# Expert results in seven places, the last sums of batch 0 behind the values, and gathers that begin two turns sooner, on one Trainium2 core

## The chip, the cores and the metric

The kernel runs on one NeuronCore of one Trainium2 chip, as one program with one launch. The metric is the device time in microseconds from the start to the end of an execution; less is better. The engines are TensorE (PE in the profile, with PEld for its weight loads), VectorE (DVE), ScalarE (ACT), GpSimd (POOL) and SyncE (SP), which only issues transfers. Each engine works its own instructions off in the order in which the program hands them over, and waits at the head of its queue for the semaphores of the instruction there. Transfers (DMA) are issued from SP, ACT and POOL; those issued from POOL here are indirect ones, in which a table of indices in on-chip memory names the row of each partition.

## What is computed

Two layers on an input of 2 images, 256 channels and 56 x 56 places (3136 tokens an image), all in float32. The first is a grouped non-local block. The second, which takes most of the time, is causal attention with four heads and then a mixture of experts in which each token takes its best two of eight:

```python
# layer 1, t: tokens (2, 3136, 256)
t = t + attention(layernorm(t), W_attn, W_proj)      # causal, 4 heads of 64

def _L1_ffn_ref(x, gate_w, gate_b, W1, b1, W2, b2):  # x = layernorm(t)
    logits = xf @ gate_w + gate_b
    probs = jax.nn.softmax(logits, axis=-1)
    top2_vals, top2_idx = jax.lax.top_k(probs, 2)
    cw = jnp.zeros((N, Ee), dtype=xf.dtype).at[jnp.arange(N)[:, None], top2_idx].add(top2_vals)
    def step(acc, params):
        w1, bb1, w2, bb2, we = params
        h = jax.nn.gelu(xf @ w1 + bb1, approximate=False)
        y = h @ w2 + bb2
        return (acc + we[:, None] * y, None)

t = t + ffn(layernorm(t))
x = _from_tokens(t, x)                               # back to (2, 256, 56, 56)
```

The hidden width of an expert is 512.

## The kernel before

**Attention.** For each batch b, stripe i of 448 query columns (seven of them) and pair of heads hp (two), the loop goes over chunks j of 128 keys. Step n computes the scores (`scores`, L806 on TensorE), ScalarE takes their exponential (L810), VectorE adds the results up into a tile `acc` (L829), and three steps later (LAG) `values(n - LAG)` multiplies them by the values into the PSUM tile `yp` (L857). When a stripe is finished, ScalarE copies `yp` out (L867) and POOL adds its halves (L868). `sum_rows` multiplies `acc` by ones (tile `sp`, L878) to get the row sums of the softmax; `store_sums` copies them (L889), sends them to memory and asks for their inverses four steps later. A table `visits` says at which step the sums of each stripe are taken. At every stripe but the first, the sums stand ahead of `values` in the order of the instructions, and `values` then copies `yp` into the `acc` tile that the sums have just been read from; for a stripe whose sums are not yet taken the copy goes to a tile of the tag "st" instead, of which there are five. The banks of `yp` are shared by the stripes, so the next stripe's values wait for the copy.

**The experts.** The 2 x 3136 x 2 pairs of token and expert are sorted by expert into 105 blocks of 128 slots, of which 102 can be filled (MAIN). Blocks 0 to 41 hold tokens of batch 0 alone; 42 to 56 hold tokens of both batches (MIXED is 57); 57 to 101 hold tokens of batch 1. Turn n of the loop works on several blocks at once: `hidden(n)` (16 matmuls, L1673, and ScalarE's GELU, L1682), `inputs` (transposes, L1650), `weights` (a copy of the expert's first matrix by VectorE, L1661), and `outputs` of the block three turns back (8 matmuls into `yp`, L1692; two VectorE additions of the bias into `ys`, L1702). The three last blocks are brought closer: two turns back and then one.

`ys` is one of three tiles of pool `es` that the blocks take in turn. For blocks below 57 SP sends it to the table `y_slots` (L1707). For blocks 42 to 98, POOL scatters its rows to `y_tokens` (L1713), by tokens of batch 1. The last three blocks (99 to 101) keep `ys` on the chip: TensorE places them with a matrix of ones and zeros, `hots` (L1784), which is made with one POOL iota for each block (L1854) and compared later.

**The finish.** Two generators run beside the experts and give one step at a time when they are pulled; the function `meanwhile` pulls them once in each turn. `finish(0)` brings batch 0's tokens together after block 56: `fetch` loads the rest of the sum for a pair of 128-token chunks (SP, L1871) and issues four gathers out of `y_slots` (POOL, L1878), `add` makes four VectorE additions (L1913), and `store` transposes the pair on TensorE (`yo`, L1927), copies it on ScalarE into one of two tiles `ot` (L1932) and sends it to the output (SP, L1933). 25 chunks take 50 gathers. `gathered[0]` counts the gathers of the present turn and is set back in each turn; `since` is the turn in which the generator began. `finish(1)` goes ahead of it in the queue and does the same for batch 1 with plain loads (L1898) out of `y_tokens`. `last_rows` loads the last rows of batch 1 (L1752); `store_last` (L1803) sends what the last three blocks placed.

The pool `bg` holds attention's row buffers, two each of the tags "xr" and "xn". Their last users are the early rows that the experts' blocks 0 to 5 read.

The order within each engine is the order of the program text, as the schedule is manual: what stands first in the code stands first in its queue.

Of the kernel before, what the change touches and what calls it, by code (L numbers as in the profile page):

```python
# [10 lines left out]
F32 = mybir.dt.float32  # L11
# [17 lines left out]
def conv_attn_moe_kernel(  # L29
# [51 lines left out]
    nc = tc.nc  # L81
    P = 128
    B, C, N = x.shape
    NH = C // P
# [9 lines left out]
    NB = N // W  # L94
# [11 lines left out]
    OFF = 16 * N  # L106
# [4 lines left out]
    GB = 3  # L111
# [9 lines left out]
    LAST = max(n for n in range(NCH) if complete(n) <= DIRECT)  # L121
    REST = N - LAST * P
# [65 lines left out]
    with tc.tile_pool(name="c_w", bufs=1) as cw, tc.tile_pool(name="c_s", bufs=2) as cs, tc.tile_pool(  # L188
        name="c_big", bufs=5, space=PSUM
    ) as cbig, tc.tile_pool(name="c_acc", bufs=1, space=PSUM) as cacc:  # L190

        xr = [cw.tile([P, NCH, C + 2], F32, name=f"xr{b}") for b in range(B)]
# [8 lines left out]
        for b in range(B):  # L201
            for col in (0, C + 1):
                nc.gpsimd.memset(xr[b][:, :, col : col + 1], 1.0)
            n = 0
# [54 lines left out]
        def channels():  # L259
# [12 lines left out]
            base=0, pattern=[[-D, G], [0, D]], channel_multiplier=1,  # L272
# [3 lines left out]
            base=D - 1, pattern=[[D, G], [0, D]], channel_multiplier=-1,  # L276
# [234 lines left out]
    def layer1(nm, general):  # L511

        with ExitStack() as whole:
# [195 lines left out]
            def attend(qT, kT, v, fst, fs, psc, py, open_batch, visit, between, clock, later, finished):  # L709
# [240 lines left out]
                for n in range(len(steps) + LAG):  # L950
                    copy_sums = None
                    if n in visits:
                        visit(*visits[n])
                        b, i, hp = visits[n]
                        if i == 0 and hp + 1 == NH:
                            turn_rows(b, 1)
                        if i > 0 and visits[n] != final:
                            copy_sums = sum_rows(b, hp, i)
                        aligned()
                    if n + 1 < len(steps) and n > LAG and steps[n][2] == 0 and steps[n - LAG - 1][2] == 0 and steps[n - LAG - 1][4]:  # L960
                        if steps[n][1] > 1:
                            turn_rows(*steps[n][:2])
                    if n < len(steps):
                        b, i = steps[n][:2]
                        if n == 0 or steps[n - 1][0] != b:
                            open_batch(b)
                        between(b, i, ends[b, i] - n, (steps[n][3] + 1) * P > i * W + 1, room(n))

                    late = n >= LAG and steps[n - LAG][4]
                    if n >= LAG:  # L970
                        due(clock[0])
                        clock[0] += 1
                    if n >= LAG and not late:
                        values(n - LAG)
                    if n in visits and visits[n][1] == 0:
                        copy_sums = sum_rows(b, hp, 0)
                    if copy_sums:
                        copy_sums()
                    if n < len(steps):
                        scores(n)  # L980
                    if late:
                        values(n - LAG)
# [595 lines left out]
            def experts(w1s, w2s, b2s, ex, es, ps6, between, amid, need, written, settle, decide):  # L1578
# [108 lines left out]
                def outputs(n, state):  # L1687
                    g, to = state
                    e = ids[n]
                    yp = ps6.tile([P, 512], F32, tag="yp", bufs=2, name=f"yp_{nm}_{n}")  # L1690
                    for k in range(KH):
                        nc.tensor.matmul(  # L1692
                            yp[:, :C],
                            g[:, k, :],
                            w2s[k][:, bass.ds(e, 1), :].rearrange("p e d -> p (e d)"),
                            start=(k == 0),
                            stop=(k == KH - 1),
                        )
                    ys = es.tile([P, C], F32, tag="ys", name=f"ys_{nm}_{n}")
                    for c in range(NH):  # L1700
                        part = slice(c * P, (c + 1) * P)
                        nc.vector.tensor_tensor(  # L1702
                            ys[:, part], yp[:, part],
                            b2s[c][:, bass.ds(e, 1), :].rearrange("p e d -> p (e d)"), ALU.add,
                        )
                    if n < MIXED:
                        nc.sync.dma_start(out=y_slots[n * P : (n + 1) * P], in_=ys)  # L1707
                    if n >= FULL0:
                        if n >= DIRECT:
                            direct[n] = ys  # L1710
                            worked[0] = n + 1
                            return
                        s = nc.gpsimd.indirect_dma_start(  # L1713
                            out=y_tokens,
                            out_offset=bass.IndirectOffsetOnAxis(
                                ap=to[:, n % GB : n % GB + 1], axis=0
                            ),
                            in_=ys,
                            in_offset=None,
                            bounds_check=2 * N - 1,  # L1720
                            oob_is_err=False,
                        )
                        group = f"y_tokens_{nm}"
                        tc.declare_no_dep(s.ins, group=group, reason="different rows")
                        tc.add_to_no_dep_group(group, s.ins)
                        scattered.append((n, s.ins))
                    worked[0] = n + 1
                    if n == MIXED - 1:
                        written()
# [119 lines left out]
                        ids.extend(experts_of(len(ids) // GB))  # L1849
                    between()  # L1850

            def number_columns(a):

                nc.gpsimd.iota(  # L1854
                    hots[a], pattern=[[1, REST]], base=LAST * P - OFF, channel_multiplier=0,
                    allow_small_or_imprecise_dtypes=True,
                )

            def finish(b, oy, bufs):

                t = ts[b]
# [1 line left out]
                def fetch(n, m, k):  # L1863

                    ys = [
                        oy.tile([P, 2, C], F32, tag=f"y{b}{c}", bufs=bufs, name=f"y{c}_{nm}{b}_{n}")
                        for c in range(2)
                    ]
                    res = oy.tile([P, 2, C], F32, tag="res", bufs=bufs + 1, name=f"res_{nm}_{n}")
                    rows = res[:k, :m]  # L1870
                    nc.sync.dma_start(out=rows, in_=rest_d[:k, n : n + m])  # L1871
                    ahead.append((n, m, k, ys, rows))
                    for c, y in enumerate(ys):
                        for a in range(m):
                            while gathered[0] == (1 if turn[0] < since + 4 else 2 - (turn[0] % 4 == 0)) or turn[0] < since + 2:
                                yield False
                            gathered[0] += 1
                            nc.gpsimd.indirect_dma_start(  # L1878
                                out=y[:k, a],
                                out_offset=None,  # L1880
                                in_=y_slots,
                                in_offset=bass.IndirectOffsetOnAxis(
                                    ap=idxs[b][:k, c, n + a : n + a + 1], axis=0
                                ),
                                bounds_check=MIXED * P - 1,
                                oob_is_err=False,
                            )
                            yield True
# [48 lines left out]

                ahead, added, since = deque(), None, turn[0]
                parts = deque(pairs())
                steps = deque(range(GB))  # L1940
                if b:
                    parts = deque([(0, 1, P), *pairs(1, LAST)])
                while b == 0 and (parts or ahead):
                    if parts:
                        yield from fetch(*parts.popleft())
                        if len(parts) % 2 == 0 and steps:
                            number_columns(steps.popleft())
                    if len(ahead) == bufs or not parts:
                        now = ahead.popleft()
                        yield from add(*now)  # L1950
                        if added:
                            while stored[0]:
                                yield False
                            store(*added)
                            yield True
                        added = now
# [296 lines left out]
            with ExitStack() as moe:  # L2253
# [23 lines left out]
                def written():  # L2277
                    spread_rows.close()
                    oy = pool(moe, "oy", bufs=2, side="right")
                    last_pool.append(oy)  # L2280
                    hot = pool(moe, "hot", bufs=1, side="right")
                    hots.extend(hot.tile([P, REST], F32, name=f"hot{a}_{nm}") for a in range(GB))
                    queue.append(finish(0, oy, 2))
                    queue.appendleft(finish(1, oy, 3))

# [203 lines left out]
```

## Time and profile before

| What | us |
|---|---|
| median of three runs | 1267.23 |
| their least and greatest | 1265.88, 1269.42 |
| the profiled execution | 1266.76 |
| its span, first to last instruction | 1264.9 |

The profile comes from one execution; its span leaves out what lies ahead of the first instruction and behind the last, 1.9 us here. The granted TensorE clock is 0.999 of full speed on the mean. The share of each slice (a fortieth of the span, 31.6 us) that an engine was busy, in tenths:

```profile
PE   8999999999999999999999999999999999999997
DVE  2582567666676574566677888785744443455563
ACT  0255555565656555465555656563334333343432
POOL 1103231110021103211111656000266012666650
DMA  9996101000000000100000223641344433556653
```

Batch 0's attention ends near 475 us, batch 1's near 850; then come the experts. POOL's busy slices 23 to 25 and 29 to 31 hold the scatters of tokens to x_slots, batch 0's and then batch 1's. POOL's busy stretch near the end (slices 35 to 39, from about 1075 us) holds the gathers of batch 0.

The windows view gives the busy time of each engine in a stretch (the columns are the stretch, its length, and for each engine its busy time with the number of instructions, then the granted clock, the share of the DMA engines and GB/s). The first is with one scatter a block, the second the first eight turns with gathers, the third the rest of them:

```profile
1020.00:1077.00 57.00, 57.00 (x399) 53.85 (x399) 21.87 (x64) 21.02 (x75) 14.58 (x15) 1.00 0.37 108
1077.00:1107.00 30.00, 30.00 (x210) 28.07 (x209) 12.60 (x36) 10.89 (x40) 19.25 (x18) 1.00 0.52 158
1107.00:1210.00 103.00, 99.13 (x698) 91.69 (x697) 59.13 (x160) 42.35 (x138) 69.40 (x65) 1.00 0.67 206
```

A line of the waits reads: engine, what it did next, its line, what ended the wait, then us in total, times, and the longest. In the timeline a row is the start, the time it took, the engine, line, operation, what it writes and reads, how often, and in brackets the idle time before it with its releaser.

### The profile page before, as it was taken

To read this page: it belongs to the slowest core of one execution; us is meant where nothing else is said; L and a number is where in the kernel's file an instruction comes from. 1 tells how busy PE (TensorE), PEld (TensorE's weight loads), DVE (VectorE), ACT (ScalarE), POOL (GpSimd) and SP (SyncE) were. 2 spreads that over 40 slices of the span, in tenths; PEclk is the share of its full clock that TensorE was granted. 3 is DMA by queue.
4 is the path that set the end of the run, shared out by engine and by line. 5 is a ranking of instruction groups with operands and counts; after the bars stand their busy time and mean duration, and the time that the engine had idled before them with its cause. 6 is when DMAs were issued, how large, how long until landed. Compare 5 with 4: busy or idle time off the path is not lost.

```text
span 1264.9 us, 28755 instructions
## 1 busy us (share of the span) xinstructions
PE 1242.6 (98%) x10881; PEld 848.1 (67%) x10881; DVE 772.8 (61%) x1687; ACT 610.7 (48%) x1237; POOL 348.9 (28%) x318
## 2 busy tenths in 40 slices
PE   8999999999999999999999999999999999999997
PEld 8876655555454545655555444479889999988886
DVE  2582567666676574566677888785744443455563
ACT  0255555565656555465555656563334333343432
POOL 1103231110021103211111656000266012666650
PEclk9999999999999999999999999999999999999999
DMA  9996101000000000100000223641344433556653
GB/s 316 352 344 194 28 24 38 25 15 26 14 17 16 1 26 21 35 23 13 9 16 25 72 67 115 218 119 60 101 143 148 121 106 92 161 180 207 208 169 116
DMA packets 119875, 125.93 MB, mean 100 GB/s; under 512 B 28375, under 2 KB 109640, under 8 KB 119730
## 3 DMA queue, kind: packets, MB, share of 16 engines
q1 hardware_dynamic: 109074, 97.45, 25.3%
q0 software_dynamic: 9840, 25.67, 6.1%
q8 instruction: 90, 1.47, 0.5%
q10 hardware_dynamic: 816, 0.88, 0.2%
q14 instruction: 55, 0.45, 0.1%
HBM read 62.06 MB, written 61.05 MB: 97 GB/s over the span
## 4 chain that ended last, share of the span: by engine, by line
PE 47%; DVE 2%; issue 1%; ACT 0%; DVEq 0%
PE ht_f L1673 14%; PE yp_f L1692 13%; PE sc_f L806 7%; PE yp_f L857 7%; PE tp_f L1650 2%; PE pp_f L682 1%; PE yo_f L1927 1%; DVE y_f L1913 1%; PE qk_f L613 1%; PE v_f L628 0%; PE tail_f L1784 0%; DVE acc_f L829 0%; PE sp_f L878 0%; ACT st_f L810 0%; PE bp_f L1405 0%
## 5 line engine op out<-in xcount | busy, mean ns | idle before, releaser
L810 ACT ACTIVATE st_f<-sc_f 128x896 f32<-128x896 f32 (+5 forms) x400 | 331.2, 839 | 189.7 <-PE sc_f L806 164.4
L829 DVE TENSOR_TENSOR acc_f<-acc_f,st_f 128x896 f32<-128x896 f32 (+6 forms) x344 | 343.9, 1000 | 105.3 <-ACT st_f L810 93.2
L806 PE MATMUL sc_f<-qT_f,kT_f 64*64 64x448 f32 (+5 forms) x3136 | 345.3, 499 | 0.5 <-issue 0.3
L857 PE MATMUL yp_f<-st_f,v_f 64*64 64x448 f32 (+4 forms) x2896 | 323.5, 511 | 1.1 <-ACT acc_f L867 0.6
L806 PEld LDWEIGHTS sc_f<-qT_f,kT_f 64*64 64x64 f32 x3136 | 140.7, 133 | 133.6 <-issue 108.1
L1682 ACT ACTIVATE g_f<-ht_f,b1b 128x128 f32<-128x128 f32 x408 | 116.5, 371 | 226.1 <-PE ht_f L1673 111.4
L857 PEld LDWEIGHTS yp_f<-st_f,v_f 64*64 64x64 f32 x2896 | 122.5, 133 | 129.1 <-issue 105.0
L1673 PE MATMUL ht_f<-xT_f,w_f 128*128 128x128 f32 x1600 | 196.2, 275 | 4.0 <-issue 3.9
L1673 PEld LDWEIGHTS ht_f<-xT_f,w_f 128*128 128x128 f32 x1600 | 192.8, 192 | 8.8 <-issue 4.7
L1537 POOL DMA_INDIRECT x_slots<-xr_f,idx x100 | 113.6, 1136 | 148.4 <-DVE xr_f L1535 75.0
L868 POOL TENSOR_TENSOR qT_f<-acc_f 128x448 f32<-128x448 f32 x22 | 25.5, 1161 | 380.3 <-ACT acc_f L867 380.2
L1661 DVE COPY w_f<-w1s_f 128x1024 f32 x102 | 71.4, 701 | 86.0 <-PE ht_f L1673 38.6
L584 POOL TENSOR_SCALAR xn_f<-t 128x256 f32<-128x256 f32 (+1 forms) x50 | 80.3, 1613 | 130.0 <-DVE t L185 44.1
L1713 POOL DMA_INDIRECT y_tokens<-ys_f,to_f x57 | 59.6, 1046 | 126.4 <-DVE ys_f L1702 100.8
L1702 DVE TENSOR_TENSOR ys_f<-yp_f,kT_f 128x128 f32<-128x128 f32 x102 | 29.4, 289 | 96.6 <-PE yp_f L1692 63.6
L613 PE MATMUL qk_f<-px_f,wat 128*128 128x512 f32 (+2 forms) x224 | 87.2, 541 | 0.6 <-ACT px_f L605 0.6
L613 PEld LDWEIGHTS qk_f<-px_f,wat 128*128 128x128 f32 x224 | 40.6, 190 | 39.7 <-issue 33.7
L1692 PE MATMUL yp_f<-w2s_f,g_f 128*128 x204 | 60.9, 379 | 0.5 <-issue 0.5
L1692 PE MATMUL yp_f<-px_f,g_f 128*128 x204 | 61.1, 381 | 0.0
L1878 POOL DMA_INDIRECT y_f<-y_slots,idx x50 | 56.6, 1132 | 15.3 <-issue 15.3
L1692 PE MATMUL yp_f<-kT_f,g_f 128*128 x204 | 60.7, 379 | 0.0
L1692 PE MATMUL yp_f<-v_f,g_f 128*128 x204 | 60.7, 379 | 0.0
(299 smaller groups left out, 1308.0 us busy)
## 6 DMA issues: line engine op xcount, KB each, us to landing
x_slots<-fill SPq DMA_DIRECT2D x1, 8190.0 KB
xb_f<-x_slots SPq DMA_DIRECT2D x60, 130.0 KB
x_slots<-fill SPq DMA_DIRECT2D x1, 7296.0 KB
y_slots<-ys_f SPq DMA_DIRECT2D x57, 128.0 KB
kept<-t SPq DMA_DIRECT2D x2, 3200.0 KB
x<-in_x_dram SPq DMA_DIRECT2D x14, 448.0 KB
rb_f<-inverses SPq DMA_DIRECT2D x56, 112.0 KB
y_f<-y_tokens SPq DMA_DIRECT2D x23, 256.0 KB
```

Of the source, the lines that this page charges most:

```text
L584: nc.gpsimd.tensor_scalar(xn[:k, a], ts[b][:k, n + a, :C], ts[b][:k, n + a, MEAN : MEAN + 1], ts[b][:k, n + a, RSTD : RSTD + 1], ALU.subtr ...
L613: nc.tensor.matmul(ps[:, :w], wat[:, c, d0 : d0 + P], px[:, s % 2, c, :w], start=(c == 0), stop=(c == NH - 1),)
L806: nc.tensor.matmul(to, left, right, start=True, stop=True)
L810: nc.scalar.activation(st[rows, :, c0:], ps[rows, :, c0:W], AF.Exp, scale=SCALE)
L829: nc.vector.tensor_tensor(acc[rows, :, c0:], acc[rows, :, c0:], st[rows, :, c0:], ALU.add)
L857: nc.tensor.matmul(to, left, right, start=first, stop=end)
L1537: s = nc.gpsimd.indirect_dma_start(out=xds[b], out_offset=bass.IndirectOffsetOnAxis(ap=idxs[b][:kk, k, n : n + 1], axis=0), in_=xr[:kk], i ...
L1661: nc.vector.tensor_copy(w, w1s[:, :, bass.ds(e, 1), :].rearrange("p c e h -> p c (e h)"))
L1673: nc.tensor.matmul(ht[:, k, :], w[:, c, k * P : (k + 1) * P], xT[:, c, :], start=(c == 0), stop=(c == NH - 1),)
L1682: nc.scalar.activation(g[:, k, :], ht[:, k, :], AF.Gelu, bias=b1bs[b][:, k, i : i + 1])
L1692: nc.tensor.matmul(yp[:, :C], g[:, k, :], w2s[k][:, bass.ds(e, 1), :].rearrange("p e d -> p (e d)"), start=(k == 0), stop=(k == KH - 1),)
L1713: s = nc.gpsimd.indirect_dma_start(out=y_tokens, out_offset=bass.IndirectOffsetOnAxis(ap=to[:, n % GB : n % GB + 1], axis=0), in_=ys, in_o ...
```

## The change

It has four parts.

1. In attention, the sums of (batch 0, stripe 6, second pair of heads) are put behind `values(n - LAG)`, as those of stripe 0 already are. So at that stripe the copy of `yp` no longer goes to the `acc` tile but to one of tag "st".
2. `ys` goes round seven places, by the block's number modulo 7: the three tiles of tag "ys", the two of tag "xr" and the two of tag "xn".
3. The gathers of batch 0 begin in the first turn instead of the third. For eight turns there is one a turn, and then one and two in turn; before there were, after two turns without, one a turn for two turns, and then two a turn, but one in each fourth. The number of gathers is the same.
4. The three iotas that number the columns of `hots` are issued together where the pool is opened, behind block 56's outputs, rather than between the gathers.

No matmul, addition or transfer is added or removed. Since later gathers mean later additions, the transposes and stores of batch 0's pairs 20, 22 and 24 move, too. At the end the order of transfers in SP's queue is, before and after (rows of batch 1 have odd numbers, of batch 0 even ones):

```
before  ... out 20, out 22, out 24, load 17 x2, out 15, last rows x4, load 19 x2, out 17, hot
after   ... rest 24, load 17 x2, out 15, last rows x4, load 19 x2, out 20, out 22, out 17, out 24, hot
```

The transposes of 20 stand ahead of `hidden(100)`, those of 22 ahead of `hidden(101)`, and those of 24 behind those of 17. The last gathers stand between the scatters of blocks 95 and 96.

```diff
@@ attend
-                        if i > 0 and visits[n] != final:
+                        short = i == 0 or (i, hp) == (NB - 1, NH - 1)
+                        if i >= 0 and not short:
                             copy_sums = sum_rows(b, hp, i)
...
                     if n >= LAG and not late:
                         values(n - LAG)
-                    if n in visits and visits[n][1] == 0:
-                        copy_sums = sum_rows(b, hp, 0)
+                    if n in visits and short and visits[n] != final:
+                        b, i, hp = visits[n]
+                        copy_sums = sum_rows(b, hp, i)
                     if copy_sums:
                         copy_sums()
@@ outputs
-                    ys = es.tile([P, C], F32, tag="ys", name=f"ys_{nm}_{n}")
+                    home = n % 7
+                    ys = (es if home < 3 else bg).tile(
+                        [P, C], F32, tag="ys" if home < 3 else "xr" if home < 5 else "xn", name=f"ys_{nm}_{n}"
+                    )
@@ finish
-            def number_columns(a):
-
-                nc.gpsimd.iota(
-                    hots[a], pattern=[[1, REST]], base=LAST * P - OFF, channel_multiplier=0,
-                    allow_small_or_imprecise_dtypes=True,
-                )
...
-                            while gathered[0] == (1 if turn[0] < since + 4 else 2 - (turn[0] % 4 == 0)) or turn[0] < since + 2:
+                            while gathered[0] == (1 if turn[0] < since + 8 else 1 + turn[0] % 2):
                                 yield False
...
-                        if len(parts) % 2 == 0 and steps:
-                            number_columns(steps.popleft())
@@ written
-                    hots.extend(hot.tile([P, REST], F32, name=f"hot{a}_{nm}") for a in range(GB))
+                    for a in range(GB):
+                        hots.append(hot.tile([P, REST], F32, name=f"hot{a}_{nm}"))
+                        nc.gpsimd.iota(
+                            hots[a], pattern=[[1, REST]], base=LAST * P - OFF, channel_multiplier=0,
+                            allow_small_or_imprecise_dtypes=True,
+                        )
                     queue.append(finish(0, oy, 2))
```

More of the change, by code (lines that the diff above doesn't have):

```diff
@@ L1939, in finish @@
                 parts = deque(pairs())
-                steps = deque(range(GB))
                 if b:
```

## The prediction

> **What bounds the kernel now.** I read the profile in the order busy line, chain of waits, idle time per engine, then the timeline at the four places that the change touches. Busy line, chain of waits and four lines of the costliest groups:
>
> ```profile
> PE 1242.6 (98%) x10881; PEld 848.1 (67%) x10881; DVE 772.8 (61%) x1687; ACT 610.7 (48%) x1237; POOL 348.9 (28%) x318
> ...
> PE 47%; DVE 2%; issue 1%; ACT 0%; DVEq 0%
> ...
> L1713 POOL DMA_INDIRECT y_tokens<-ys_f,to_f x57 | 59.6, 1046 | 126.4 <-DVE ys_f L1702 100.8
> L1702 DVE TENSOR_TENSOR ys_f<-yp_f,kT_f 128x128 f32<-128x128 f32 x102 | 29.4, 289 | 96.6 <-PE yp_f L1692 63.6
> ...
> L1878 POOL DMA_INDIRECT y_f<-y_slots,idx x50 | 56.6, 1132 | 15.3 <-issue 15.3
> ```
>
> TensorE is busy 98% of the span. The reader is to see that a change which adds and removes no matmul can win only out of TensorE's idle time: 1264.9 - 1242.6 = 22.3 us, part of it the start and the drain after the last matmul. The lines that name what ended it, in the waits of TensorE:
>
> ```profile
> PE yo_f L1927 <- DVE y_f L1913: 4.2, 7, 1.2
> PE ht_f L1673 <- issue: 3.9, 5, 1.0
> PE gram L317 <- POOL blocks L270: 3.1, 1, 3.1
> PE qk_f L613 <- ACT px_f L605: 0.6, 1, 0.6
> PE yp_f L857 <- ACT acc_f L867: 0.6, 1, 0.6
> ```
>
> The columns are us in total, times, longest. `gram` lies at the start, `qk_f` in the projections, and the `ht_f` gaps at 912 to 974 us in the scatters of x_slots: out of the change's reach. Two lines are in reach: 4.2 us before `yo_f` (with a gap put down to issue it is 4.6) and 0.6 us before `yp_f` at the change of batch.
>
> **Part 1, batch 0's last sums behind the values.** The timeline there:
>
> ```profile
> 473.17 0.59 PE L878 MATMUL sp_f<-acc_f,ones_t 128*32 128x224 f32 x8
> ...
> 473.68 0.98 PE L857 MATMUL yp_f<-st_f,v_f 64*64 64x448 f32 x8
> ...
> 474.73 0.91 ACT L867 COPY acc_f<-yp_f 128x896 f32<-128x896 f32 x1 [0.64 <-PE yp_f L857]
> ...
> 475.69 1.51 PE L857 MATMUL yp_f<-st_f,v_f 64*64 64x448 f32 x16 [0.59 <-ACT acc_f L867]
> ```
>
> The sums (0.51 us from start to the next start) stand before the batch's last values; ScalarE copies those values out, and TensorE stands 0.59 us because the next values need that bank. With the sums behind, the values and the copy begin 0.51 us sooner; ScalarE has been idle 0.64 us by then, so it can follow. Of 0.59 us about 0.08 stays: **-0.5 us**, and TensorE is the bound, so the end moves with it. The copy now goes to a tile of the scores' ring of five instead of the acc tile; one turn of that ring is later by a step. No wait of the scores on that ring shows, so 0; its ends are 0 and +0.5. The sums' own ScalarE copy (0.35 us) follows with POOL and DMA work whose next reader is four steps on.
>
> **Part 2, seven places for `ys`.** Nothing is computed more or less. `ys` for block m+3 must wait until the DMA of block m has read its tile. In the trace the writes to y_slots land a median 1.7 us after issue (at most 4.4), the scatters to y_tokens 2.1 to 5.6; a block takes 3.73 us, three blocks 11.2. The smallest margin anywhere is 4.3 us. So the wait that seven places could remove is not there: **0**. Where `ys` begins late in the gathers' stretch (up to 2.9 us after its product), ScalarE's GELU and the weight copies begin late in the same blocks, and these do not touch the three tiles. The four borrowed tiles are last used by early rows at blocks 0 to 5, so they add no wait beyond those blocks; ends 0 and +0.3.
>
> **Part 3, the gathers' rate and start.** 50 gathers, none left out. Before: none for two turns, one a turn for two, then 1.75 a turn, so the last falls in turn 30. After: one for eight turns, then 1.5, so (50 - 8)/1.5 = 28 more, turn 36 of 43. With the one scatter that each block issues, POOL carries 2.75 indirect DMAs a block before, 2.0 and then 2.5 after. One takes 1.05 to 1.13 us, and 0.30 of issue follows a gather (15.3/50): POOL is nearly full before and has about 0.4 us a block spare after. What this is worth shows here, at TensorE's longest gap:
>
> ```profile
> 1114.43 1.02 POOL L1713 DMA_INDIRECT y_tokens<-ys_f,to_f  x1 [0.91 <-DVE ys_f L1702]
> 1114.64 0.48 DVE L1913 SCALAR_TENSOR_TENSOR y_f<-y_f,t 128x256 f32<-128x256 f32 x1 [0.50 <-issue]
> ...
> 1115.70 0.33 PE L1927 MATMUL yo_f<-ident,y_f 128*128 128x128 f32 x1 [1.16 <-DVE y_f L1913]
> ```
>
> The four additions of a pair (0.48 each) start late on VectorE, and the transposes stand behind them on TensorE. They are late because VectorE and ScalarE answer TensorE up to 3 us late where indirect DMAs are dense; no view names the cause. Between 1020 and 1077 us, with one scatter a block, TensorE is busy 57.00 of 57.00 us; from 1107 to 1210 it is busy 99.13 of 103. The gain lies between all of it (-4.6, if the lower rate is enough) and a loss of +3 (six more turns with gathers at half a microsecond a turn, which is the dense stretch's worst rate). By density, linearly between one a block (no gap) and 2.75 (4.6 us): 4.6 x (2.5 - 1)/(2.75 - 1) = 3.9. I take **-0.7**, since the number of pairs that TensorE transposes is the same.
>
> Here the Trainium skill (SBUF — State Buffer, section "SBUF: two separate sides") speaks against making a dense stretch longer: a DMA issued from GpSimd cannot write its descriptors while VectorE runs an fp32 SBUF copy. Such a copy, the weights' at L1661 (701 ns), runs in every block. In the trace the 22 gathers that touch one in time took 1.25 us on the mean, the 28 others 1.04. By the rule a gather would lose up to the whole copy, 0.7 us, and 50 gathers up to 35 us of POOL; by the row 0.21 each. The row counts, and the same 50 gathers meet the same copies, so neither changes my sum; by the rule POOL's spare 0.4 us a block would be gone and the gain with it.
>
> **Part 4, iotas ahead of the gathers.** Three of 518 ns on POOL, now together behind block 56, ahead of the first gather and of scatter 57: 1.6 us. The first gather waits for block 56's write, which lands at 1074.9 us (issued 1073.21, 1.7 later), and scatter 57 is ready near 1076.9: the wait hides them. Without that cover they cost POOL 1.6 us once, and nothing on TensorE. **0**.
>
> **Part 5, the end.** The later gathers carry batch 0's last pairs (20, 22, 24) into the last turns. Their transposes move from idle-free blocks to idle-free blocks: 0 on TensorE. But on SP their stores now stand behind the two loads of rows 19, which wait for a buffer. The view is the timeline of the end:
>
> ```profile
> 1250.75 0.88 SPq L1898 DMA_DIRECT2D y_f<-y_tokens  x2
> ...
> 1252.03 0.38 SPq L1933 DMA_DIRECT2D out_dram<-ot_f  x1
> ...
> 1257.41 0.60 PE L1927 MATMUL yo_f<-ident,y_f 128*128 128x128 f32 x4
> ...
> 1258.05 0.59 ACT L1932 COPY ot_f<-yo_f 128x512 f32<-128x512 f32 x1 [0.66 <-PE yo_f L1927]
> ...
> 1258.66 0.38 ACTq L1933 DMA_DIRECT2D out_dram<-ot_f  x1
> ```
>
> The output tile `ot` has two places. Store 20 is issued near 1251.7; L later it lands, tile 17 is copied and stored (0.8), L later that lands, and only then may tile 19 be copied, due at 1258.05. So 1251.7 + 2L + 0.8 must not pass 1258.05: L at most 2.77 us, and each microsecond above costs two. Nearest row: store 17 took 2.85 us (1252.03 to 1254.88), so **+0.2**; its ends are 0 (most stores 2.0 to 2.8) and +3.3 (three stores took up to 4.4). Behind ScalarE's waiting copy stand tile 24's copy and the first `hot` copy (1256.86), reached only with L over 4. The Trainium skill (DMA: Bandwidth & Descriptors, "Anatomy of one DMA — SWDGE (gpsimd) path") fits 2.0 us plus bytes/436e3, my estimate for 256 KB being 2.6: by that rule, made for another queue, the chain just fits and costs 0. I take the row.
>
> **Sum.** -0.5 + 0 - 0.7 + 0 + 0.2 = **-1.0 us**. The profiled execution took 1266.76 us (span 1264.9), 0.5 below the median of the runs shown, 1267.23; on that median the forecast is **1266.2**.
>
> **Rivals.** What a measurement can tell here from no change is 0.3%, 3.8 us, so 1263.4 to 1271.0.
>
> 1. Forecast, next to nothing: 1263.5 to 1268.5, most likely 1266.2. Chance 0.70. For it: TensorE 98% busy, no wait on `ys`. Against it: unexplained lateness.
> 2. The gaps before `yo_f` go: the lower rate brings VectorE back on time, 4.6 + 0.5 = 5.1 us, so 1262.1. For it: no gap at one scatter a block. Against it: the rate falls only from 2.75 to 2.5. Chance 0.14.
> 3. Slower, by the ring of two at the end: stores 20 and 17 each land late. It decides from L = 2.77; at 4.4 it is +3.3, with tile 24 and `hot` behind it some +4.5, less 0.5 from part 1: 1271.2. For it: the end's loads and stores share the queue. Against it: most stores need under 2.8. Chance 0.12.
> 4. The change does not do what it says: seven places remove no wait and the gathers' gaps stay as they are: -0.5 + 0.2, 1266.9. Chance 0.04, inside the forecast's range.
>
> Faster by over 0.3%: 0.14; within: 0.73; slower: 0.13. The range takes in case 1 and 4 and the near halves of 2 and 3: 1262.5 to 1270.0.
>
> **What would show it.** Part 1: the gap of 0.59 before `yp_f` L857 near 475 us is under 0.15. Part 2: in the stretch with one scatter a block `ys` begins as before. Part 3: the waits of TensorE show `yo_f <- DVE y_f` near 3.5 us; under 1 is case 2, over 5 proves the spreading harmful. Part 4: the first gather still begins near 1075. Part 5: in the timeline of the end tile 19's copy starts within 0.5 us after its transposes; a wait on a landing store there is case 3. Wrong altogether would be a new gap in TensorE before 1000 us other than part 1's.

## The result, and the profile after

The changed kernel takes 1260.06 us (median of 7 runs, 1259.61 to 1264.03), the kernel before 1267.23 (7 runs, 1265.34 to 1270.32): a ratio of 0.9951, with a 95% interval of 0.9934 to 0.9967. That is 7.2 us faster, where 1.0 was forecast and the range ended at 1262.5. The profiled execution took 1262.54 us (span 1260.8), 2.5 over its median. So the two profiles are 4.2 us apart and the medians 7.2. In the profile of after, blocks 0 to 42 take 167.7 us, 2.5 more than in that of before. The granted clock was 0.97 there from 912 to 980 us (1.00 before), which I estimate at 68 x 0.03 = 2.0 us; but e4_three, described below, took 167.4 us for the same blocks at a clock of 1.00, so the clock isn't shown to be the cause.

The busy line of after, and the waits of TensorE (us in total, times, longest):

```profile
PE 1242.5 (99%) x10881; PEld 848.9 (67%) x10881; DVE 775.5 (62%) x1687; ACT 610.3 (48%) x1237; POOL 346.9 (28%) x318
```

```profile
PE ht_f L1675 <- issue: 3.8, 8, 0.9
PE gram L317 <- POOL blocks L270: 3.0, 1, 3.0
PE yo_f L1925 <- DVE y_f L1911: 0.7, 2, 0.3
PE qk_f L613 <- ACT px_f L605: 0.6, 1, 0.6
```

The wait of 4.2 us before `yo_f` is 0.7, and the 0.6 before `yp_f` at the change of batch has left the list. There the timeline of after has

```profile
472.71 0.98 PE L857 MATMUL yp_f<-st_f,v_f 64*64 64x448 f32 x8
473.62 0.59 PE L878 MATMUL sp_f<-acc_f,ones_t 128*32 128x224 f32 x8
473.76 0.91 ACT L867 COPY both_f<-yp_f 128x896 f32<-128x896 f32 x1
...
474.72 1.51 PE L857 MATMUL yp_f<-st_f,v_f 64*64 64x448 f32 x16
```

The values come first, the copy runs beside the sums, and the next values have no idle time in brackets.

The gathers' stretch at the same places, in the windows view (the stretch, its length, busy time and count of PE, PEld, DVE, ACT, POOL, the granted clock, DMA share, GB/s):

```profile
1077.00:1107.00 30.00, 29.90 (x210) 28.14 (x209) 12.88 (x36) 11.29 (x41) 18.65 (x18) 1.00 0.51 156
1107.00:1210.00 103.00, 102.69 (x729) 96.36 (x728) 58.57 (x161) 42.34 (x140) 64.20 (x60) 1.00 0.65 201
```

TensorE is busy 102.69 of 103 us where it was 99.13, and does 729 matmuls there instead of 698: it is ahead.

The gathers' real start and pace differ from the numbers in the code. The first gathers, in the kernel before and then in the changed one:

```profile
1082.20 1.37 POOL L1878 DMA_INDIRECT y_f<-y_slots,idx  x1 [0.30 <-issue]
```

```profile
1079.38 1.34 POOL L1876 DMA_INDIRECT y_f<-y_slots,idx  x1 [2.12 <-issue]
```

Counted from the start of block 57, that is 20.9 and 17.2 us: the sooner start in the code is worth one block of 3.73 us, not two. And counted in POOL's order between one scatter and the next, the 50 gathers take 34 turns before and 40 after. In the dense part (behind the first two turns with gathers before, behind the first eight after) there are 1.5 a turn before, where the code's limit averages 1.75, and 1.31 after, where it averages 1.5. With the scatter, POOL so carries 2.5 and 2.3 indirect transfers a block.

What the end gives back shows in its timeline:

```profile
1245.78 0.88 SPq L1896 DMA_DIRECT2D y_f<-y_tokens  x2
...
1246.70 5.42 SPq L1931 DMA_DIRECT2D out_dram<-ot_f  x4
...
1250.62 0.93 ACT L1930 COPY ot_f<-yo_f 128x512 f32<-128x512 f32 x2 [7.36 <-DMA out_dram<-ot_f]
...
1252.90 0.60 PE L1925 MATMUL yo_f<-ident,y_f 128*128 128x128 f32 x4
...
1255.09 0.58 ACT L1930 COPY ot_f<-yo_f 128x512 f32<-128x512 f32 x1 [2.21 <-DMA out_dram<-ot_f]
```

Tile 17's copy waits for store 20, and the last copy for store 17. It is due at 1253.54 and starts at 1255.09.

### The profile page after: what moved, and what is told of

The parts are those of the page before. It is cut to its first block, busy times and chain, and to the rows that moved or that the text cites. A ratio compares the mean times of both kernels' runs of the same rounds, so it can differ in the third digit from the quotient of the medians.

```text
span 1260.8 us, 28740 instructions
## 1 busy us (share of the span) xinstructions
PE 1242.5 (99%) x10881; PEld 848.9 (67%) x10881; DVE 775.5 (62%) x1687; ACT 610.3 (48%) x1237; POOL 346.9 (28%) x318
## 4 chain that ended last, share of the span: by engine, by line
PE 47%; DVE 1%; issue 1%; DMA 1%; ACT 0%; DVEq 0%; SPq 0%; ACTq 0%
PE ht_f L1675 14%; PE yp_f L1694 14%; PE sc_f L806 7%; PE yp_f L857 7%; PE tp_f L1652 2%; PE pp_f L682 1%; PE yo_f L1925 1%; PE qk_f L613 1%; DMA out_dram<-ot_f 1%; PE v_f L628 0%; DVE y_f L1911 0%; DVE acc_f L829 0%; PE sp_f L878 0%; PE bp_f L1407 0%; ACT st_f L810 0%
```

## Experiments

The runs fell on several chips, and the same kernel before took 1264 to 1267 us on some and 1251 on others. I call the first **late** chips and the second **quiet** ones; what is late on them is shown below. The table holds three stretches out of the traces: from the start of block 62's first hidden matmul to block 97's, from there to the last matmul, and on to the end of the span. A transpose that moves from the first to the second changes both and not their sum. The first two together are 171.1 or 171.2 us in every trace from a quiet chip, and 178.1 in the kernel before on its late one.

| Kernel | Chip | blocks 62 to 97 | to the last matmul | to the span's end |
|---|---|---|---|---|
| before | late | 146.1 | 32.0 | 6.9 |
| after | late | 139.8 | 32.9 | 7.3 |
| e1_rate | late | 138.3 | 32.9 | 7.4 |
| e2_seven | late | 143.7 | 32.0 | 5.9 |
| e3_sums | late | 145.1 | 32.0 | 6.0 |
| e4_three | late | 138.3 | 32.9 | 7.5 |
| h0_plain | late | 139.2 | 32.0 | 6.0 |
| h1_two | late | 148.7 | 31.5 | 6.1 |
| f1_start | quiet | 139.5 | 31.6 | 6.1 |
| f2_pace | quiet | 138.3 | 32.9 | 7.0 |
| f4_two | quiet | 139.6 | 31.5 | 6.1 |
| g0_after | quiet | 138.3 | 32.9 | 6.8 |
| g1_ot3 | quiet | 138.3 | 32.9 | 6.5 |

**Each part by itself, on a late chip** (before 1263.89 us, 23 runs). The gathers alone:

```diff
-while gathered[0] == (1 if turn[0] < since + 4 else 2 - (turn[0] % 4 == 0)) or turn[0] < since + 2:
+while gathered[0] == (1 if turn[0] < since + 8 else 1 + turn[0] % 2):
```

> The kernel before with the gathers' rate and start alone (part 3). Theory 'rate': it carries the gain, 4 to 6.5 us faster than before, and TensorE's waits show yo_f <- DVE y_f at 1 us or less instead of 4.2. Theory 'places': VectorE is late because ys waits for a free tile, so the rate alone brings 2 us or less and the yo_f waits stay above 2.5 us.

Measured: 1258.24 us, a ratio of 0.9952 (0.9936 to 0.9968), and no wait of `yo_f` on VectorE is left. The seven places alone:

```diff
-ys = es.tile([P, C], F32, tag="ys", ...)
+home = n % 7
+ys = (es if home < 3 else bg).tile([P, C], F32, tag="ys" if home < 3 else "xr" if home < 5 else "xn", ...)
```

> The kernel before with seven places for ys alone (part 2). Theory 'rate': no change, within 1.5 us of before, yo_f <- DVE y_f near 4.2 us and ys as late behind its product as before (up to 2.9 us). Theory 'places': 3 us or more faster, ys no longer late, yo_f waits under 2 us.

Measured: 0.9995 (0.9982 to 1.0008). Its profile is of its fastest execution, 1259.43 us with a median of 1262.80. The `yo_f` waits come to 2.4 us in it, fewer than in the profile of before, but the times do not follow, and `ys` is still late by up to 2.5 us. The sums alone:

```diff
-if i > 0 and visits[n] != final:
+short = i == 0 or (i, hp) == (NB - 1, NH - 1)
+if i >= 0 and not short:
     copy_sums = sum_rows(b, hp, i)
...
-if n in visits and visits[n][1] == 0:
-    copy_sums = sum_rows(b, hp, 0)
+if n in visits and short and visits[n] != final:
+    b, i, hp = visits[n]
+    copy_sums = sum_rows(b, hp, i)
```

> The kernel before with batch 0's last sums behind the values alone (part 1). Both theories: the gap of 0.59 us before yp_f at the change of batch is gone, 0.5 us faster, which the times can hardly tell; the yo_f waits stay near 4.2 us. If it is over 2 us faster, the prediction missed something in attention.

Measured: 0.9999 (0.9988 to 1.0011). The gap of 0.59 is gone in the trace; the times can't tell 0.5 us. And the changed kernel with three places again:

```diff
-home = n % 7
-ys = (es if home < 3 else bg).tile([P, C], F32, tag="ys" if home < 3 else "xr" if home < 5 else "xn", ...)
+ys = es.tile([P, C], F32, tag="ys", ...)
```

> The changed kernel with three places for ys as before (part 2 undone). Theory 'rate': as fast as the changed kernel, 5.5 to 7.5 us faster than before, yo_f waits under 1.2 us. Theory 'places': 3 us or more of the gain is lost.

Measured: 0.9960 (0.9944 to 0.9975). Part 3 carries the gain, and the seven places carry none of it that can be measured (the interval of e2_seven leaves room for 2.3 us won or 1.0 lost). e1_rate keeps the iotas between the gathers and has the whole gain, so part 4 isn't needed for it.

**Pace or start.** f1_start begins in the first turn at the old pace, f2_pace keeps the old start and takes the new pace, f4_two lifts the limit to two in every turn. By the count between scatters f4_two is hardly denser: 1.6 gathers a turn in the dense part, for 1.5 before, not the 2 that its expectation takes for granted.

```diff
f1_start  +while gathered[0] == (1 if turn[0] < since + 4 else 2 - (turn[0] % 4 == 0)):
f2_pace   +while gathered[0] == (1 if turn[0] < since + 4 else 1 + turn[0] % 2) or turn[0] < since + 2:
f4_two    +while gathered[0] == (1 if turn[0] < since + 4 else 2) or turn[0] < since + 2:
```

> The kernel before with the gathers begun in the first turn instead of the third, at the old pace (one for four turns, then 1.75 a turn). Theory 'pace': the stretch stays as dense, so under 2.5 us faster than before, TensorE's gaps at yo_f stay at 2.5 us or more and the additions of ys are late by up to 2.5 us or more. Theory 'start': the sooner start is what frees the late turns, 4 us or more faster.

> The kernel before with the old start (none for two turns, one for two), then the new pace of 1.5 a turn. Theory 'pace': 4 to 6.5 us faster, yo_f waits under 1 us, ys late by at most 2 us. Theory 'start': under 2.5 us faster.

> The kernel before with two gathers in every turn after the fourth, none left to one in each fourth turn. Theory 'pace': denser than before (3 indirect transfers a block), so the gaps at yo_f are 5 us or more and the time is 0 to 4 us over before's. Theory 'start': the gathers end sooner, so the same or faster.

Measured, against 1250.84 us for the kernel before (33 runs): f1_start 0.9995 (0.9986 to 1.0004), f2_pace 1.0007 (0.9998 to 1.0016), f4_two 0.9997 (0.9988 to 1.0007). None of the theories had foreseen a chip on which the kernel before is 13 to 16 us faster. Here nothing is late: at the old pace TensorE is without a gap from block 62 on. f1_start and f2_pace were run twice more, as i1 and i2 and as j1 and j2:

> The kernel before with the gathers begun in the first turn, at the old pace. On a chip where the kernel before takes 1262 us or more: theory 'pace', under 2.5 us faster, gaps and short hold-ups at yo_f still over 3 us in blocks 62 to 97; theory 'start', 4 us or more faster. Where it takes some 1251: within 1 us of it.

> The kernel before with the old start and the new pace of 1.5 a turn. On a chip where the kernel before takes 1262 us or more: theory 'pace', 4 to 6.5 us faster, no gap over 1 us in all before yo_f, ys late by at most 2 us; theory 'start', under 2.5 us. Where it takes some 1251: 0 to 1.5 us slower, through the stores at the end.

> The sooner start alone, at the old pace, a third time. If the kernel before takes 1262 us or more here: theory 'pace', under 2.5 us faster, and blocks 62 to 97 take 143 us or more; theory 'start', 4 us or more faster. If it takes some 1251: within 1 us, and the question stays open.

> The new pace alone, with the old start, a third time. If the kernel before takes 1262 us or more here: theory 'pace', 4 to 6.5 us faster, blocks 62 to 97 in 140 us or less; theory 'start', under 2.5 us faster. If it takes some 1251: 0 to 1.5 us slower, and the question stays open.

Both fell on quiet chips again (before 1250.52 and 1250.66 us, 21 runs each). The start gave 0.9999 (0.9990 to 1.0008) both times; the pace 1.0006 (0.9997 to 1.0015) and 1.0007 (0.9998 to 1.0017). Each interval of the pace takes in 1, but the three medians are 0.9 to 1.3 us over before's, as its longer end in the table would have it. Which of the two brings the gain on a late chip **stays open**: no run of the one without the other fell on one. That the start moves the first gather by only one block speaks for the pace, but doesn't show it.

What lateness is, shows in one block. First the kernel before on its late chip, block 70:

```profile
1110.65 1.95 PE L1673 MATMUL ht_f<-xT_f,w_f 128*128 128x128 f32 x16
...
1113.66 0.29 DVE L1702 TENSOR_TENSOR ys_f<-yp_f,kT_f 128x128 f32<-128x128 f32 x1 [2.89 <-PE tp_f L1650]
1113.82 1.14 ACT L1682 ACTIVATE g_f<-ht_f,b1b 128x128 f32<-128x128 f32 x4 [2.00 <-PE tp_f L1650]
...
1115.70 0.33 PE L1927 MATMUL yo_f<-ident,y_f 128*128 128x128 f32 x1 [1.16 <-DVE y_f L1913]
...
1116.62 0.55 PE L1927 MATMUL yo_f<-ident,y_f 128*128 128x128 f32 x3 [0.59 <-DVE y_f L1913]
```

And the same block of j1_start, with the same two gathers in the turn, on a quiet chip:

```profile
1102.49 1.95 PE L1673 MATMUL ht_f<-xT_f,w_f 128*128 128x128 f32 x16
1102.69 0.29 DVE L1702 TENSOR_TENSOR ys_f<-yp_f,kT_f 128x128 f32<-128x128 f32 x1 [1.14 <-PE yp_f L1692]
...
1104.48 1.14 ACT L1682 ACTIVATE g_f<-ht_f,b1b 128x128 f32<-128x128 f32 x4 [2.33 <-PE ht_f L1673]
...
1106.22 0.60 PE L1927 MATMUL yo_f<-ident,y_f 128*128 128x128 f32 x4
```

GELU follows the hidden matmuls' start by 1.99 us on the quiet chip, by 3.17 on the late one; `ys` comes 0.20 us after that start, or 3.01. Two engines that wait for the same sender are late together, and the releaser named on the late chip is a later instruction of TensorE than the one waited for. The waits view sums this up: before on its late chip, then j1_start.

```profile
ACT g_f L1682 <- PE ht_f L1673: 111.4, 52, 4.8
...
ACT g_f L1682 <- PE tp_f L1650: 35.0, 15, 4.1
ACT g_f L1682 <- remote: 26.7, 5, 8.8
```

```profile
ACT g_f L1682 <- PE ht_f L1673: 217.6, 101, 4.1
```

One and the same wait is put down to the right releaser 101 times on the quiet chip, and to several, "remote" among them, on the late one.

The changed kernel was profiled on both kinds of chip, so it can be compared with itself. In blocks 62 to 96 GELU is later than its 1.99 us by up to 3.24 us in the profile of after (mean 0.91), and in g0_after in none of them. A rival is that VectorE gets its instructions late, whatever they wait for. It doesn't fit: the additions of the finish (`y_f`, `res_f`), which wait for no matmul, have 3.1 us of idle time ahead of them in blocks 62 to 97 of after, and 6.0 in g0_after. So what is late is the start of work that waits for TensorE. I read it as a late signal, since the matmuls that follow on TensorE start on time; whether it is late in being sent or in being seen, the traces don't tell.

**Indirect transfers or bytes.** Each gather becomes a plain load of 128 KB in SP's queue; batch 0's tokens then get other rows than theirs.

```diff
-nc.gpsimd.indirect_dma_start(out=y[:k, a], in_=y_slots, in_offset=..., ...)
+r = (2 * (n + a) + c) * P
+nc.sync.dma_start(out=y[:k, a], in_=y_slots[r : r + k])
```

It ran three times, as f3_plain, g2_plain and h0_plain. The first two fell on quiet chips, with ratios of 1.0001 (0.9992 to 1.0010) and 1.0002 (0.9993 to 1.0011), and leave the question open:

> The kernel before with each of the 50 gathers replaced by a plain load of as many rows (128 KB) in SP's queue, so that batch 0's tokens get other experts' rows; the turns stay the same. Theory 'indirect': what makes VectorE late is the indirect transfers on POOL, so ys is late by under 0.3 us in most blocks and no gap stands at yo_f: 4 to 7 us faster. Theory 'traffic': the bytes moved make it late, so ys stays late by 2 us and more and the gaps stay near 4 us.

> The kernel before with each gather replaced by a plain load of as many rows in SP's queue, batch 0's tokens getting other rows, once more. If this chip shows the lateness: theory 'indirect', ys late by under 0.3 us in nearly all blocks from 62 to 97 and the time 4 to 7 us under before's; theory 'traffic', ys late by 2 us and more, and the gaps before yo_f stay. If the chip does not show it: no change, within 1 us.

The third, and the limit of two a turn with it, fell on a late chip (before 1267.37 us, 14 runs):

> The kernel before with each gather replaced by a plain load of as many rows in SP's queue (batch 0's tokens get other rows). On a chip where the kernel before takes 1262 us or more: theory 'indirect', ys late by under 0.3 us in nearly all blocks from 62 to 97, 4 to 7 us faster; theory 'traffic', late by 2 us and more, gaps before yo_f as before. On a chip where it takes some 1251: no change within 1 us.

> The kernel before with two gathers in every turn after the fourth. Where the kernel before takes 1262 us or more: theory 'pace', 0 to 4 us slower, gaps before yo_f of 5 us or more; theory 'start or end', the same or faster, since the gathers end sooner. Where it takes some 1251: no change within 1 us.

h0_plain: 1260.72 us, 0.9948 (0.9929 to 0.9966). `ys` is never late by more than 0.10 us in blocks 59 to 93, and the windows show no idle time of TensorE at as many bytes as before:

```profile
1107.00:1210.00 103.00, 103.00 (x737) 97.17 (x736) 63.38 (x173) 44.84 (x144) 26.55 (x28) 1.00 0.69 209
```

209 GB/s against 206 before: it isn't the bytes. Without the gathers the one scatter a block is harmless even there. So on a late chip it is the gathers, as indirect transfers that GpSimd issues on top of the scatters, that make the other engines answer TensorE late. The edit changes the issuer, the table of indices and the order of the rows at once; which of these matters was not separated.

h1_two: 1.0001 (0.9986 to 1.0016). Blocks 62 to 97 take 148.7 us, the longest of all, but this doesn't show that a denser pace is worse. The pace is 1.6 for 1.5, and the granted clock was lower in the trace:

```profile
1170.00:1190.00 20.00, 20.00 (x134) 18.84 (x135) 10.83 (x29) 9.44 (x31) 12.67 (x12) 0.91 0.60 187
```

By my estimate that alone is 20 x 0.09 = 1.8 of the 2.6 us over before's 146.1. Theory "pace" missed the gaps as well:

```profile
PE ht_f L1673 <- issue: 4.5, 8, 1.1
PE yo_f L1927 <- DVE y_f L1913: 2.9, 4, 1.3
```

Before `yo_f` they come to 2.9 us, less than before's 4.2 and not 5 or more; all idle time of TensorE from block 62 on is 5.6, against 4.6. Its time, 0.1 us over before's, lies at the edge of what the theory named.

**The change again, and the end.**

> The changed kernel again, on whichever chip this is. The last two sets of runs were on two chips: on the first the kernel before took 1264 us and ys was late, on the second 1251 us and nothing was late. Theory 'lateness': the gain follows it. If the kernel before takes some 1262 us or more here, 4.5 to 7.5 us faster; if it takes some 1251, between 0.5 us faster and 1.5 us slower. Rival 'robust': faster by 4 us or more on either.

Measured on a quiet chip (before 1250.65 us, 33 runs): 1251.18, 1.0003 (0.9994 to 1.0012). Theory "lateness" holds and "robust" falls: the change that saves 7 us on one chip saves nothing here. With a third tile for the output:

```diff
-ot = oy.tile([P, NH, 2 * P], F32, tag="ot", bufs=2, ...)
+ot = oy.tile([P, NH, 2 * P], F32, tag="ot", bufs=3, ...)
```

> The changed kernel with three tiles ot instead of two. In the changed kernel's profile the last copy of ot waits 2.2 us for a store. Theory 'ring': it then starts within 0.7 us of its transposes, and the time is 0.8 to 1.6 us under the changed kernel's of the same call; no wait on out_dram<-ot_f is left on ScalarE. Rival 'queue': the stores themselves are late in SP's queue, so under 0.3 us.

Measured: 1250.89 us, 0.9999 (0.9990 to 1.0008), 0.3 us under g0_after, which these intervals can't tell from nothing. The timelines of the end, g0_after and then g1_ot3:

```profile
1244.04 0.58 ACT L1930 COPY ot_f<-yo_f 128x512 f32<-128x512 f32 x1 [1.60 <-DMA out_dram<-ot_f]
1244.66 0.38 ACTq L1931 DMA_DIRECT2D out_dram<-ot_f  x1
```

```profile
1242.19 0.59 ACT L1930 COPY ot_f<-yo_f 128x512 f32<-128x512 f32 x1 [0.66 <-PE yo_f L1925]
...
1242.81 0.38 ACTq L1931 DMA_DIRECT2D out_dram<-ot_f  x1
```

The wait on the ring is gone, as "ring" said: after the last matmul the last store is issued 0.7 us later instead of 1.6. But from that issue to the end of the span it is now 5.9 us instead of 5.1, so 0.2 of 0.9 is kept: theory "ring" had the wait right and the gain wrong. The last store is now issued 1.2 and 0.4 us behind the two `hot` ones, where it was 2.2 and 1.3; that they share the way is a possible reason, and was not tested. g3_two, the limit of two a turn once more, gave 1.0000 (0.9991 to 1.0010) on this chip:

> The kernel before with two gathers in every turn after the fourth, once more. If this chip shows the lateness: theory 'pace', 0 to 4 us slower than before, with gaps before yo_f of 5 us or more. If it does not: no change, within 1 us.

## Why the prediction was wrong

**The step that failed is the size of part 3**, "By density, linearly between one a block (no gap) and 2.75 (4.6 us)", from which -0.7 was taken. What the runs showed:

- The dependence isn't linear. A transpose waits only if VectorE is later than the room it has. Without gathers (h0_plain) the addition into `ys` begins 0.87 to 0.97 us behind the end of its product; what goes beyond 0.87 I count as its lateness. In blocks 59 to 93 the worst fell from 2.84 us to 1.95, the mean from 0.94 to 0.65 (0.42 in e1_rate), and that was enough for nearly all waits to go: 4.6 us of idle time before `yo_f` from block 62 on became 0.7, and none in e1_rate. That was rival 2, at 0.14, put at 1262.1; the reason against it, that the pace falls "only from 2.75 to 2.5", was the same mistake. GELU's lateness did not fall in the changed kernel (mean 0.85 us before, 0.91 after), but no wait of TensorE on GELU shows in either profile.
- The room was only just enough. In block 70 of e1_rate the last addition ends 0.04 us ahead of the transposes that read it:

```profile
1111.06 0.48 DVE L1913 SCALAR_TENSOR_TENSOR y_f<-y_f,t,y_f 128x256 f32<-128x256 f32 x1
...
1111.58 0.60 PE L1927 MATMUL yo_f<-ident,y_f 128*128 128x128 f32 x4
```

- The densities were the code's limits. By the count above they are 2.5 and 2.3 indirect transfers a block, not 2.75 and 2.5, and the last gather falls six and four turns later than the prediction's 30 and 36. That is not what failed: the same straight line gives 4.6 x 1.31/1.5 = 4.0 us left, -0.6. "POOL is nearly full" doesn't hold either: it is busy 69.4 of 103 us in the dense stretch before, by estimate 81 with 0.30 us of issue for each of some 38 gathers. And since start and pace were not parted on a late chip, it isn't shown that the density, and not the start, took the lateness away.
- The pool was too small as well. I read 4.6 us out of the idle time before `yo_f`. A set of four transposes that runs through is busy 0.60 us, but one that is held up counts 0.33 for the first and 0.55 for the others, as in block 70 of the kernel before. From block 62 to the last matmul TensorE is busy 173.5 us before and 171.1 in e1_rate, for the same matmuls: the other 2.3 us of what was won were booked as work. So this stretch is 6.9 us shorter in e1_rate (178.1 to 171.1), and 5.4 in the changed kernel's profile; the end gives 0.4 back.
- The forecast did not know that the lateness belongs to the chip. The line in the rivals, "Against it: unexplained lateness", named the hole without a price. On a quiet chip nothing is won (g0_after, 1.0003).

**Point by point.** Part 1 was right: -0.5 of 0.59 was forecast, and the gap is gone in the trace; the times can't confirm 0.5 us. Part 2 was right: 0, within the noise, from both sides by e2_seven and e4_three. Part 4 at 0 fits, since the three iotas end 2.1 us ahead of the first gather, and was not run by itself; but its sign, a first gather near 1075, was wrong for both kernels (1082.2 and 1079.4). Part 5 had the right mechanism, ring and queue, and a term too small: +0.2 from a store of 2.85 us, where in the changed kernel 3.9 us each go by from the issue of stores 20 and 17 to the copy that waits for them. By its own chain, 1246.70 + 3.92 + 0.61 + 3.86 = 1255.09, as measured; the copy is 1.55 late. The end from the last matmul is 0.4 us longer than before in these two profiles, but some 0.9 in those of quiet chips (6.0 to 7.0) and 1.3 in those of late ones when the kernel before's own profile is left out (6.0 to 7.4). The estimate of 2.6 us that the prediction worked out from the Trainium skill (DMA: Bandwidth & Descriptors, "Anatomy of one DMA — SWDGE (gpsimd) path") was further off than the row; its fit is for transfers that GpSimd issues, and these are SP's.

On the rule that GpSimd is locked out while VectorE copies (Trainium skill, SBUF — State Buffer, "SBUF: two separate sides"): gathers beside a weight copy took 1.24 us in e1_rate and 1.05 otherwise, and on a quiet chip (f1_start) 1.21 and 1.02. The mean hides that the traces come near the rule: a gather that began with 0.40 us of the copy left took 1.29 us in e1_rate, one with 0.56 left 1.46. As the lengthening is there on both kinds of chip, it isn't by itself what sets the late ones apart.

## What to carry to other kernels

A wait that several engines show together, with changing releasers behind one sender, points to a late signal rather than to a missing buffer; here a change of the gathers' timing took most of the wait away and more places did not. Count what an engine really issues in the trace, since a limit in the code is not a pace. When the consumer has a fixed room, a small cut of the lateness can remove the whole wait, so a straight line through two densities is no estimate: compare the lateness with the room. And run such a change on more than one chip, since the gain may be only the cure of one chip's trouble.

## What the hardware showed unexpectedly

- Chips differ by 1.1 to 1.3% in the time of the unchanged kernel: 1264 and 1267 us where TensorE's signals are answered late, 1251 on four others. The gathers' stretch is only part of it (from block 62 to the last matmul 178.1 us before, 171.1 in f1_start). On the quiet chips the scatters to x_slots leave no gap either: from 912 to 980 us TensorE is idle 4.5 us before on its late chip and not at all in f1_start, and blocks 0 to 42 take 165.2 and 159.3 us. What in a chip does it, no run here shows.
- Durations of the indirect transfers on GpSimd are alike on both: gathers 1.13 us on the mean in the kernel before (late), 1.11 in f1_start (quiet). So the transfers' own time on GpSimd doesn't tell a late chip from a quiet one.
